# Channel attention and selective scan: the next image's statistics taken in the v stretch, its factors and key weights moved forward, B loaded ahead of C, one square per piece

## The chip, the cores and the metric

The kernel runs on one core of one Trainium2 chip. The time is the device time of one execution in microseconds. Three runs of the kernel before gave 19570.98, 19573.84 and 19581.24 us; the median, 19573.84, is the time before. The core has five engines that run their own instruction streams in order: PE (matmul), DVE (vector), ACT (activation), POOL (GpSimd) and SP, which here issues the DMAs.

## What is computed

The input x is 8 images of 384 channels and 64 x 64 positions (L = 4096), in float32. Two layers with residuals follow one another; the whole reference, cut to what matters:

```python
x = x + attention(gn(x))      # gn: 32 groups of 12 channels, over positions too
x = x + scan_layer(gn(x))

def attention(x):             # wq, wk, wv, wproj: 1x1; dw*: 3x3 for each channel
    q, k, v = (dwconv(conv1x1(x, w), dw) for ...)
    q, k = l2norm(q), l2norm(k)                      # over positions
    attn = softmax(q @ k.T * temperature)            # 8 heads, 48 x 48 each
    return conv1x1(attn @ v, wproj)

def scan_layer(x):            # 4 directions, 16 states for each channel
    dt, B, C = split(x_proj @ direction(x))
    dt = softplus(dt_proj @ dt + dt_bias)
    h[l] = h[l-1] * exp(dt * A) + dt * x * B
    y = sum over states of h * C, + D * x            # merged over directions
    return gelu(layernorm_over_channels(y) * ln_w + ln_b)
```

## The kernel before, in words

The images run one after the other (L1232): `channel_attention(b)`, then `selective_scan(b)`. The last part of an image, layer norm, gelu and residual, is done inside the next image's attention (`finishing`, L187), and for the last image at the end (`finish`). Channels are three blocks (NJ = 3) of 128 partitions. Most compute instructions are pinned: each engine executes them in the order in which they are written. DMAs are not pinned; a scheduler places them on SP's queue, and SP executes that queue in order.

**Attention.** Work is cut into 36 pieces (w, m, p): 12 of k, 12 of q (block m, then quarter p of 16 rows), 12 of v (quarter p, then block m); KQ = 24 is the number of the first v piece. The loop at L645 is a software pipeline over t: PE makes the bands of piece t+2 (L364, L368), ACT and POOL start and end the sum of piece t+1 (L416, L423), DVE finishes piece t with five taps and an addition (`finish_sum`, L440), and a finished k or q piece t-1 is transposed (`to_tokens`, L461). There ACT copies the transposes out of PSUM and squares the half piece with a running sum into `ssq` (L475). From t = KQ + 3 on the v stretch also projects: `project_in` (L595) on PE and `project_out` (L604) on DVE: add to x, take statistics, store x1. What is still to be projected after the loop is done at L736. `bank` (L341) hands out four PSUM banks in turn.

**Norms.** Group norm is folded into the weights: `norm_factors` (L131) aggregates batch statistics, averages mean and then variance over groups by two sets of seven matmuls with one column (L143), and ends with Sqrt on ACT and a reciprocal. `scale_weights` (L256) scales a weight matrix by rstd; `shift_of` (L263) makes a bias by nine matmuls with one column.

**Scan.** It has S = 32 steps (4 directions x 8 chunks of 512 positions), each UN = 12 units (3 blocks x 4 groups of 4 states), U = 384 units. In a unit ACT makes four decays (`decay`, L890, in three PSUM banks), POOL makes the product dt x B (`drive`, L903), DVE scans four states (`scan`, L913), PE transposes the result (`turn`), ACT copies it out (`keep`), PE multiplies by C (`add_up`). For every step PE projects x to dt, B and C (`project`, L802), and `lay_out` (L815) stores B and C to DRAM and loads C back in another shape (`cx`, four DMAs); `fetch` (L852) loads B to all partitions, one DMA of 1 MB for each group. C is shuffled by POOL (`mingle_c`), transposed by PE (`turn_c`) and spread by DVE (`spread_c`, L844). `project` and `turn_c` use one PSUM bank, tag "m". `drive(0)` and `drive(1)` are called ahead of the first unit, and unit u calls `drive(u + 1)`.

**Look-ahead.** In the last three steps of an image's scan (not of the last image) `look_ahead` (L1030) loads the next image's x in eight parts into the tile "near", takes 24 batch statistics on DVE (L1040), runs the steps of `norm_factors`, and two units before the end scales the key weights and makes their bias (L1054). Step 31 also loads x itself for the next image (L1160).

Of the kernel before, what the change touches and what calls it, by code (L numbers as in the profile page):

```python
# [9 lines left out]
F32 = mybir.dt.float32  # L10
# [85 lines left out]
def tile_channel_attention_then_selective_scan(ctx: ExitStack, tc: tile.TileContext, a: dict):  # L96
# [33 lines left out]

    def norm_factors(pool, psum, stats, tag, bank, pin=lambda i: i, **home):  # L131

        mv = pool.tile([P, NJ, 2], F32, name=f"mv{tag}", **home)
        mean = pool.tile([P, NJ], F32, name=f"mean{tag}", **home)
        rstd = pool.tile([P, NJ], F32, name=f"rstd{tag}", **home)
        var = pool.tile([P, NJ], F32, name=f"var{tag}", **home)

        def average(name, src):
            pm = psum.tile([P, CH], F32, tag=bank, name=f"{name}{tag}")
            for j in range(NJ):  # L140
                near = [i for i in range(NJ) if abs(i - j) <= 1]
                for i in near:
                    pin(nc.tensor.matmul(  # L143
                        pm[:, j : j + 1], lhsT=avg[:, i, j * P : (j + 1) * P], rhs=src[:, i, 0:1],
                        start=i == near[0], stop=i == near[-1],
                    ))
            return pm

        for j in range(NJ):
            pin(nc.vector.bn_aggr(mv[:, j, :], stats[:, j].rearrange("p c s -> p (c s)")))  # L150
        yield
        pm = average("pm", mv)
        yield
        pin(nc.vector.tensor_copy(mean, pm[:, 0:NJ]))
        pin(nc.vector.tensor_sub(var, mv[:, :, 0], mean))
        pin(nc.vector.tensor_mul(var, var, var))
        pin(nc.vector.tensor_add(var, var, mv[:, :, 1]))
        yield
        pv = average("pv", var.rearrange("p (j o) -> p j o", o=1))
        yield  # L160
        pin(nc.vector.tensor_scalar_add(rstd, pv[:, 0:NJ], GN_EPS))
        yield
        pin(nc.scalar.activation(rstd, rstd, AF.Sqrt))
        yield
        pin(nc.vector.reciprocal(rstd, rstd))
        yield mean, rstd
# [96 lines left out]
    def shift_of(pool, psum, tag, wt, mean, name):  # L263

        pin = tc.keep_in_program_order
        pb = psum.tile([P, CH], F32, tag=tag, name=f"pb{name}")
        for m in range(NJ):
            for j in range(NJ):
                pin(nc.tensor.matmul(
                    pb[:, m : m + 1], lhsT=wt[:, j, bass.ts(m, P)], rhs=mean[:, j : j + 1],  # L270
                    start=j == 0, stop=j == NJ - 1,
                ))
        bias = pool.tile([P, NJ], F32, name=f"bias{name}")
        pin(nc.vector.tensor_scalar_mul(bias, pb[:, :NJ], -1.0))
        return bias
# [20 lines left out]
    def channel_attention(b, x, stats, before):  # L296

        pin = tc.keep_in_program_order
        with ExitStack() as st:
# [9 lines left out]
            for n in ("k", "q", "v"):  # L309
                dws[n] = wp.tile([P, NJ, 9], F32, name=f"dw{n}{b}")  # L310
                nc.sync.dma_start(dws[n], a["dw" + n])
            mask = wp.tile([P, NJ, BW], F32, name=f"mask{b}")
            nc.sync.dma_start(mask, a["mask"])
# [13 lines left out]
            kT = wp.tile([P, NT, C], F32, tag="kv", name=f"kT{b}")  # L327
            ssq = wp.tile([P, 2 * NJ, NCH], F32, name=f"ssq{b}")
            ga = wp.tile([P, NJ, BW], F32, name=f"ga{b}")
            x1_d = dram.tile([NJ, P, L], F32, tag="x1d", bufs=2, name=f"x1d{b}")  # L330
# [130 lines left out]
            def to_tokens(t, h):  # L461
# [7 lines left out]
                if w == "k":  # L469
                    out = kT[:, n : n + 4, bass.ts(m, P)]  # L470
                else:
                    out = qTs[t, h] = work.tile([P, 4, P], F32, tag="qT", name=f"qT{b}_{t}_{h}")
                pin(nc.scalar.copy(out, pt))
                i = m if w == "k" else NJ + m
                pin(nc.scalar.activation(  # L475
                    src, src, AF.Square, accum_out=ssq[:, i, 2 * p + h : 2 * p + h + 1]
                ))

# [34 lines left out]
            def norms():  # L513

                polish_root(helper, roots, var)
                rks = work.tile([P, 4, P], F32, tag="qT", name=f"rks{b}")
                spread.append(rks.rearrange("p i l -> p (i l)"))
                rks = spread[0]
# [120 lines left out]
            def fin_bank(i, n):  # L639
                return bank(f"pz{b}_{i}_{n}")  # L640

            load_w("wq")
            parts = list(range(L // FT)) if before else []
            stats_left, todo, grams, last, ready = list(parts), [], [], iter(()), []
            for t in range(-2, T):  # L645
# [48 lines left out]
                def mid(tap):  # L694
# [4 lines left out]
                    if tap in (2, 8) and ready and t > KQ + 3:  # L699
                        project_out(*ready.pop(0))  # L700

                half(0)
# [22 lines left out]
                while ready:  # L725
                    project_out(*ready.pop(0))
                if t == KQ:
                    squares()
# [4 lines left out]
                if 0 <= cc < T and pieces[cc][:2] == ("v", NJ - 1):  # L733
                    p = pieces[cc][2]
                    todo += [(m, c) for c in (2 * p, 2 * p + 1) for m in range(NJ)]
            for m, c in todo:  # L736
                project_in(m, c)
                project_out(m, c)
                next(last, None)
                next(last, None)  # L740
            all_of(last)
        return x, x1_d, stats1

    def selective_scan(b, x1, stats1):

        y_d = dram.tile([L, C], F32, tag="yd", bufs=2, name=f"yd{b}")
        with ExitStack() as st:
# [18 lines left out]
            with tc.tile_pool(name=f"sn{b}", bufs=1, reuse_waits="tile") as np_:  # L766
                mean, rstd = all_of(norm_factors(np_, ps_t, stats1, f"1_{b}", "t", pin))
                shift = np_.tile([P, NJ], F32, name=f"shift{b}")
                nc.vector.tensor_mul(shift, mean, rstd)
                nc.vector.tensor_scalar_mul(shift, shift, -1.0)  # L770
                for c in range(5):
                    for j in range(NJ):
                        s = x1[j][:, bass.ts(c, CH)]
                        if c < 1:
                            pin(nc.scalar.activation(
# [39 lines left out]
            def lay_out(s):  # L815
# [3 lines left out]
                bc_d = dram.tile([2 * N, CH], F32, tag="bcd", bufs=3, name=f"bcd{b}_{s}")  # L819
                nc.sync.dma_start(bc_d, xd[R:XR, :])  # L820
                cx = work.tile([NG * NQ, NV, HP], F32, tag="cx", bufs=1, name=f"cx{b}_{s}")
                for g in range(NG):
# [3 lines left out]
                    )  # L826
                xds[s], bc_ds[s], cxs[s] = xd, bc_d, cx

# [179 lines left out]
            for j in range(NJ):  # L1008
                step_size(0, j, step_matmul(0, j))
                weigh(0, j)  # L1010
            for g in range(NG):
                fetch(0, g)
            mingle_c(0)
            turn_c(0)
            for g in range(NG):
                spread_c(0, g)
            drive(0)
# [12 lines left out]
            def look_ahead(u):  # L1030

                i = u - (U - 3 * UN)
                if b + 1 == B or i < 0:
                    return
                n, odd = divmod(i, 2)
                if i == 0:
                    near["st"] = x_stats(b + 1)
                if not odd and 1 <= n <= NCH:
                    for j in range(NJ):
                        pin(nc.vector.bn_stats(near["st"][:, j, n - 1, :], near["x"][:, j, :]))  # L1040
                if not odd and n < NCH:
                    near["x"] = big.tile([P, NJ, CH], F32, tag="near", name=f"nx{b}_{n}")
                    nc.sync.dma_start(
                        near["x"], x_d[b + 1, :, :, bass.ts(n, CH)].rearrange("j p l -> p j l")
                    )
                if i == 2 * UN + 1:
                    near["f"] = norm_factors(big, ps_m, near["st"], f"0_{b + 1}", "m", pin)
                if i > 2 * UN:
                    r = next(near["f"], None)
                    if r:  # L1050
                        near["r"] = r
                if i == 2 * UN:
                    near["w"] = load_wk(b + 1)
                if i == 3 * UN - 2:  # L1054
                    mean, rstd = near["r"]
                    scale_weights(near["w"], rstd)
                    bias = shift_of(big, ps_m, "m", near["w"], mean, f"{b + 1}k")
                    near["r"] += near["w"], bias

# [96 lines left out]
            for u in range(U + 1):  # L1156
                look_ahead(u)
                unit(u)
                if u == U - UN + 3 and b + 1 < B:
                    x_next = load_x(b + 1)  # L1160
            add_up(U - 1, NLB - 1)
            take(S - 1, 2)
            if x_next:
                x_next = x_next, near["r"]
        return y_d, x_next
# [60 lines left out]
    with tc.tile_pool(name="pm", bufs=1, space=PSUM) as ps:  # L1226
        st0 = all_of(norm_factors(big, ps, st0, "0_0", "m"))
        wk = load_wk(0)
# [3 lines left out]
    for b in range(B):  # L1232
        x1, x1_d, stats1 = channel_attention(b, *x, before)
        y_d, x = selective_scan(b, x1, stats1)
        before = (b, x1_d, y_d)
# [50 lines left out]
```

## Time and profile before

| what | value |
| --- | --- |
| time, median of three runs | 19573.84 us (19570.98 to 19581.24) |
| profiled execution, its own time | 19593.03 us |
| span of its instructions | 19591.2 us |
| mean granted TensorE clock | 0.954 |
| DMA | 1849.25 MB, mean 94 GB/s |
| statistics of x1, L607, DVE 128x512 | 192, 694 ns each |
| statistics of the next x, L1040, DVE 128x512 | 168, 672 ns each |
| ACT table loads at L872 | 256, 1283 ns each |
| POOL product, L910, 128x2048 | 3072, 4578 ns each |
| DVE scan, L922, 128x512, with a carry | 10752, 1263 ns each |

Times are those of one profiled execution. A row of groups gives the engine, the operation, its tiles (out<-in), its count, busy time and mean duration. A row of the timeline gives the start, the duration and, in brackets, how long the engine had been idle before it and what ended that idle time. A row of windows gives each engine's busy time in a stretch.

### The profile page before, as it was taken

Reading aid. Unit: us, or ns where it says so; the run is one execution under the profiler, and the core shown is the slowest. Engines: PE = TensorE matmul, PEld = TensorE weight load, DVE = VectorE, ACT = ScalarE, POOL = GpSimd, SP = SyncE. Lnnn points to the kernel's source line nnn. Section 1 sums busy time; section 2 is a strip of 40 time slices with the busy share of each in tenths; the row PEclk is TensorE's granted clock in tenths of the full one; section 3 lists DMA queues with packets and bytes.
Section 4 is the critical chain, followed back from the end, with each engine's and each line's share of the span. In section 5 each row is a group of like instructions: output and inputs, shape, how many; then the busy total and the mean of one; then the engine's idle time right before and its main releaser. Section 6 shows DMA issues by size and latency. Waiting matters only on the chain.

```text
span 19591.2 us, 415258 instructions
## 1 busy us (share of the span) xinstructions
PE 17097.0 (87%) x166560; PEld 10219.2 (52%) x166560; DVE 18453.4 (94%) x17510; ACT 17584.1 (90%) x30011; POOL 16874.4 (86%) x7486
## 2 busy tenths in 40 slices
PE   7888888888888888888888888888888888888887
PEld 4555545555455554555545555455554555545554
DVE  7999989999899998999989999899998999989998
ACT  6999979999799987999879998899988999889998
POOL 4999959999599985999859998599985999869997
PEclk9999999999999999999999999999999999999998
DMA  1232322223222232232322323223232223322223
GB/s 47 84 97 97 112 89 83 94 97 111 91 86 94 95 109 89 87 97 96 109 85 87 97 97 108 85 87 97 97 108 92 83 95 97 106 93 88 94 93 124
DMA packets 1214410, 1849.25 MB, mean 94 GB/s; under 512 B 154209, under 2 KB 1018721, under 8 KB 1075265
## 3 DMA queue, kind: packets, MB, share of 16 engines
q1 hardware_dynamic: 1211616, 1822.57, 28.7%
q8 instruction: 1314, 21.53, 0.5%
q14 instruction: 616, 5.04, 0.1%
q10 hardware_dynamic: 864, 0.12, 0.0%
HBM read 1503.58 MB, written 318.77 MB: 93 GB/s over the span
## 4 chain that ended last, share of the span: by engine, by line
ACT 27%; PE 23%; DVE 15%; issue 4%; POOL 3%; DMA 1%; SPq 0%; DVEq 0%; ACTq 0%; POOLq 0%
ACT da L898 12%; ACT hc L949 10%; PE pt L943 10%; DVE h L922 10%; PE py L960 5%; PE px L810 3%; DVE ac L451 3%; POOL db L910 2%; ACT dt L872 1%; PE pp L599 1%; PE pd L864 1%; PE py L966 1%; ACT pr L413 1%; ACT L872 1%; ACT L898 1%
## 5 line engine op out<-in xcount | busy, mean ns | idle before, releaser
L910 POOL TENSOR_TENSOR db<-w,B 128x2048 f32<-128x2048 f32 x3072 | 14053.0, 4578 | 618.8 <-DVE h L922 514.7
L922 DVE TENSOR_TENSOR_SCAN h<-da,ca,db 128x512 f32<-128x512 f32 x10752 | 12786.6, 1263 | 305.3 <-ACT da L898 287.0
L898 ACT ACTIVATE da<-dt,neg_a 128x512 f32<-128x512 f32 x12288 | 8741.8, 713 | 157.6 <-DVE h L922 153.4
L943 PE MATMUL pt<-ident,h 128*128 128x128 f32 x49152 | 8127.0, 294 | 858.4 <-DVE h L922 505.8
L949 ACT COPY hc<-pt 128x512 f32<-128x512 f32 x12288 | 7393.0, 604 | 704.7 <-PE pt L943 641.1
L943 PEld LDWEIGHTS pt<-ident,h 128*128 128x128 f32 x49152 | 5452.3, 146 | 3314.2 <-issue 1912.0
L960 PE MATMUL py<-hc,cp 128*32 128x128 f32 x98304 | 5070.4, 290 | 893.4 <-ACT hc L949 726.0
L960 PEld LDWEIGHTS py<-hc,cp 128*32 128x32 f32 x98304 | 2050.1, 110 | 3164.5 <-ACT hc L949 1607.1
L922 DVE TENSOR_TENSOR_SCAN h<-da,db 128x512 f32<-128x512 f32 x1536 | 1748.2, 1206 | 115.8 <-ACT da L898 73.5
L420 POOL TENSOR_TENSOR pr<-pr,pr 128x1008 f32<-128x1008 f32 x288 | 673.3, 2338 | 1201.1 <-ACT pr L413 1184.0
L810 PE MATMUL px<-x,wx 128*44 128x128 f32 x6144 | 1219.8, 343 | 36.9 <-DVE cp L849 21.3
L881 POOL TENSOR_TENSOR w<-x,dt 128x512 f32<-128x512 f32 x744 | 1062.4, 1428 | 33.4 <-ACT dt L872 31.9
L810 PEld LDWEIGHTS px<-x,wx 128*44 128x44 f32 x6144 | 687.4, 128 | 367.0 <-issue 190.0
L864 PE MATMUL pd<-xd,wdt 128*128 128x512 f32 x1536 | 731.8, 613 | 157.0 <-DVE h L922 151.2
L426 POOL TENSOR_TENSOR pr<-pr,pr 128x1008 f32<-128x1008 f32 x288 | 574.8, 1996 | 277.2 <-ACT pr L413 193.8
L849 DVE TENSOR_TENSOR cp<-quad,pct 128x512 f32<-128x512 f32 x1024 | 628.2, 674 | 10.9 <-PE pct L838 10.9
L599 PE MATMUL pp<-v,mT 128*128 128x512 f32 x1152 | 539.1, 618 | 92.5 <-DVE v L456 91.4
L872 ACT ACT_TABLE_LOAD x256 | 328.4, 1283 | 229.1 <-PE pd L864 228.1
L936 POOL COPY ca<-h 128x4 f32<-128x4 f32 x2688 | 531.6, 198 | 0.0
L864 PEld LDWEIGHTS pd<-xd,wdt 128*128 128x128 f32 x1536 | 272.3, 190 | 465.4 <-issue 239.2
L872 ACT ACTIVATE dt<-pd,dt_bias 128x512 f32<-128x512 f32 x768 | 475.0, 686 | 8.2 <-PE pd L864 4.4
L1002 DVE TENSOR_TENSOR ys<-ys,py 128x512 f32<-128x512 f32 x576 | 383.9, 667 | 34.6 <-PE py L960 34.6
(334 smaller groups left out, 11500.5 us busy)
## 6 DMA issues: line engine op xcount, KB each, us to landing
B<-bcd SPq DMA_DIRECT2D x1024, 1024.0 KB, 4.8
yd<-ys SPq DMA_DIRECT2D x384, 256.0 KB, 3.4
ys<-yd SPq DMA_DIRECT2D x768, 128.0 KB, 2.9
yd<-ys SPq DMA_DIRECT2D x768, 128.0 KB, 4.3
x<-in_x SPq DMA_DIRECT2D x48, 1024.0 KB, 7.2
x1d<-x SPq DMA_DIRECT2D x192, 256.0 KB, 2.8
ys<-yd SPq DMA_DIRECT2D x192, 256.0 KB, 3.0
fy<-yd SPq DMA_DIRECT2D x128, 384.0 KB, 3.8
```

The source lines that it names most:

```text
L420: pin(nc.gpsimd.tensor_add(q[:, :, 1:], q[:, :, 1:], left[:, :, : W - 1]))
L599: pin(nc.tensor.matmul(pps[m, c], lhsT=fold_of[0][:, j, bass.ts(m, P)], rhs=vs["v"][:, j, bass.ts(c, CH)], start=j == 0, stop=j == NJ - 1,))
L810: pin(nc.tensor.matmul(split(pxs[s][:XR, :])[:, part, :], lhsT=wx[:, j, k, :], rhs=view(x1[j], k, c)[:, part, :], start=i == 0, stop=i == ...
L864: pin(nc.tensor.matmul(pd, lhsT=wdt[:, k, bass.ts(j, P)], rhs=xds[s], start=True, stop=True))
L872: pin(nc.scalar.activation(dts[s, j], pd, AF.Softplus, bias=small["dt_bias"][:, j, k : k + 1]))
L881: pin(eng.tensor_mul(split(ws[s, j]), view(x1[j], k, c), split(dts[s, j])))
L898: pin(nc.scalar.activation(t, dts[s, j], AF.Exp, scale=neg_a[:, j, steps[s][0], n : n + 1]))
L910: pin(eng.tensor_mul(t, w.broadcast_to([P, NV, CH]), bts[s, g]))
L922: pin(nc.vector.tensor_tensor_scan(h, da, db, 0.0 if start else carries[s - 1][:, j, n : n + 1], ALU.mult, ALU.add,))
L943: pin(nc.tensor.transpose(t[:, f, :], hs[u][:, bass.ts(q, HP), :].rearrange("p l v -> p (l v)"), ident))
L949: pin(nc.scalar.copy(t, pts.pop((u, lb))))
L960: pin(nc.tensor.matmul(py[f * HP : (f + 1) * HP, lb, :], lhsT=cps[s, g][:, q, :], rhs=hc[:, f, :], start=g == lb == 0, stop=g == NG - 1 an ...
```

## The change

There are six edits.

1. In the v stretch of image b, x of image b + 1 is loaded in twelve parts of 1024 columns into two tiles that have no more use by then (`qT`, and `gm`, which joins the former `mask` and `ga`), and DVE takes the statistics from there, at taps 0 and 6 of `finish_sum`.
2. The factors of image b + 1 are made step by step between the last projections of image b. `norm_factors` now keeps one operand of each small subtraction and product in PSUM.
3. The key weights of image b + 1 are loaded at unit 24 by the text, scaled at unit 41 and their bias made at unit 42. What `look_ahead` did in the last three steps is gone. The load of x itself stays.
4. At the start of the scan B's first group is loaded before C's four loads, and C is spread after unit 0.
5. The first chunk's middle block is normalised by DVE, the others still by ACT; the shift is one operation, not two.
6. A piece is squared once (1024 columns), not in two halves. The q transposes stand in one tile with two halves, where they had two buffers.

```diff
-    def norm_factors(pool, psum, stats, tag, bank, pin=lambda i: i, **home):
+    def norm_factors(pool, bank, stats, tag, pin=lambda i: i):
...
-        pin(nc.vector.tensor_copy(mean, pm[:, 0:NJ]))
-        pin(nc.vector.tensor_sub(var, mv[:, :, 0], mean))
-        pin(nc.vector.tensor_mul(var, var, var))
-        pin(nc.vector.tensor_add(var, var, mv[:, :, 1]))
+        off = pm[:, NJ : 2 * NJ]
+        pin(nc.vector.tensor_sub(off, mv[:, :, 0], pm[:, :NJ]))
+        pin(nc.vector.tensor_copy(var, off))
+        pin(nc.vector.tensor_mul(off, var, off))
+        pin(nc.vector.tensor_add(var, mv[:, :, 1], off))
+        pin(nc.vector.tensor_copy(mean, pm[:, :NJ]))
...
                 pin(nc.scalar.copy(out, pt))
-                i = m if w == "k" else NJ + m
-                pin(nc.scalar.activation(
-                    src, src, AF.Square, accum_out=ssq[:, i, 2 * p + h : 2 * p + h + 1]
-                ))
+                if h:
+                    i, src = m if w == "k" else NJ + m, piece_out(t)
+                    pin(nc.scalar.activation(src, src, AF.Square, accum_out=ssq[:, i, p : p + 1]))
...
+            ahead = [(j, c) for j in range(NJ) for c in range(0, NCH, 2)] if b + 1 < B else []
+            st0, coming = x_stats(b + 1) if ahead else None, []
+            halls = [qT.rearrange("p i l -> p (i l)"), gm[:, : 2 * CH]]
+
+            def load_ahead():
+
+                for t in halls:
+                    if ahead:
+                        j, c = ahead.pop(0)
+                        nc.sync.dma_start(t, x_d[b + 1, j, :, c * CH : (c + 2) * CH])
+                        coming.append((j, c, t))
+
+            def stats_ahead():
+
+                if coming:
+                    j, c, t = coming.pop(0)
+                    for i in range(2):
+                        pin(nc.vector.bn_stats(st0[:, j, c + i, :], t[:, bass.ts(i, CH)]))
...
+                    if tap in (0, 6):
+                        stats_ahead()
...
+                if t > KQ + 2:
+                    load_ahead()
...
+            while coming:
+                stats_ahead()
+            factors = iter(())
+            if st0:
+                factors = norm_factors(big, bank, st0, f"0_{b + 1}", pin)
+            after = None
             for m, c in todo:
                 project_in(m, c)
+                after = next(factors, after)
                 project_out(m, c)
...
+            for after in factors:
+                pass
...
-                nc.vector.tensor_mul(shift, mean, rstd)
-                nc.vector.tensor_scalar_mul(shift, shift, -1.0)
+                pin(nc.vector.scalar_tensor_tensor(shift, mean, -1.0, rstd, ALU.mult, ALU.mult))
...
-                        if c < 1:
+                        if c < 1 and j != 1:
...
                 nc.sync.dma_start(bc_d, xd[R:XR, :])
+                xds[s], bc_ds[s] = xd, bc_d
+                if s == 0:
+                    fetch(0, 0)
                 cx = work.tile([NG * NQ, NV, HP], F32, tag="cx", bufs=1, name=f"cx{b}_{s}")
...
-            for g in range(NG):
+            for g in range(1, NG):
                 fetch(0, g)
             mingle_c(0)
             turn_c(0)
-            for g in range(NG):
-                spread_c(0, g)
...
-                if not odd and 1 <= n <= NCH:
-                    for j in range(NJ):
-                        pin(nc.vector.bn_stats(near["st"][:, j, n - 1, :], near["x"][:, j, :]))
-                if not odd and n < NCH:
-                    near["x"] = big.tile([P, NJ, CH], F32, tag="near", name=f"nx{b}_{n}")
-                    nc.sync.dma_start(
-                        near["x"], x_d[b + 1, :, :, bass.ts(n, CH)].rearrange("j p l -> p j l")
-                    )
-                if i == 2 * UN + 1:
-                    near["f"] = norm_factors(big, ps_m, near["st"], f"0_{b + 1}", "m", pin)
...
-                if i == 2 * UN:
+                if u == 2 * UN:
                     near["w"] = load_wk(b + 1)
-                if i == 3 * UN - 2:
-                    mean, rstd = near["r"]
-                    scale_weights(near["w"], rstd)
-                    bias = shift_of(big, ps_m, "m", near["w"], mean, f"{b + 1}k")
-                    near["r"] += near["w"], bias
+                if u == 3 * UN + 5:
+                    scale_weights(near["w"], after[1])
+                if u == 3 * UN + 6:
+                    near["b"] = shift_of(big, ps_m, "m", near["w"], after[0], f"{b + 1}k")
...
                 unit(u)
+                if u == 0:
+                    for g in range(NG):
+                        spread_c(0, g)
```

## The prediction

> **What bounds the kernel now.** I read the page first (busy shares, chain, groups), then one image stage by stage in the table of windows, then the waits and the timelines at the four places that the change touches. I use image 2 (the third) and, as a witness, image 7 (the last), which has no next image.
>
> ```profile
> span 19591.2 us, 415258 instructions
> PE 17097.0 (87%) x166560; PEld 10219.2 (52%) x166560; DVE 18453.4 (94%) x17510; ACT 17584.1 (90%) x30011; POOL 16874.4 (86%) x7486
> 5382.40:7000.00 1617.60, 1439.37 (x15981) 879.14 (x15981) 1579.84 (x1432) 1527.99 (x2655) 1566.97 (x693) 0.97 0.29 93
> ```
> Window columns: stretch, length, busy us of PE, weight load, DVE, ACT, POOL (instructions), clock, DMA share, GB/s. Inside the scan DVE works 1579.84 of 1617.60 us: it sets the pace, POOL is close behind (1566.97), so a DVE microsecond there is a microsecond of time. An image lasts some 2438 us: keys 87, queries 107, values and projection 194, start of the scan 26, scan 2020.
>
> ```profile
> 7117.80:7189.10 71.30, 57.66 (x639) 34.26 (x631) 71.30 (x72) 62.92 (x108) 61.62 (x30) 0.98 0.46 143
> 7189.10:7255.10 66.00, 53.36 (x576) 31.71 (x575) 65.01 (x64) 57.30 (x98) 60.43 (x28) 0.97 0.42 135
> 7255.10:7330.00 74.90, 62.56 (x636) 41.22 (x634) 65.36 (x61) 59.61 (x105) 54.05 (x16) 0.83 0.29 91
> 19305.60:19367.00 61.40, 54.74 (x607) 31.99 (x607) 60.76 (x56) 58.28 (x104) 60.79 (x29) 1.00 0.31 97
> 19367.00:19429.50 62.50, 56.24 (x603) 33.37 (x599) 61.07 (x56) 58.08 (x103) 61.37 (x31) 0.95 0.31 95
> 19429.50:19487.90 58.40, 48.57 (x594) 29.10 (x592) 58.40 (x52) 55.20 (x97) 48.19 (x13) 0.97 0.09 20
> ```
> These are the last three scan steps of image 2 (71.3 + 66.0 + 74.9 = 212.2) and of image 7 (182.3). Image 7 has no look-ahead. The other six images lie between 210 and 213 by the starts of their scans.
>
> **Removed at the scan's end.** The difference, 29.7 us, is the price of the look-ahead where it stands. It agrees with its parts: 24 statistics x 0.672 = 16.1, aggregation 0.8, small operations 6.6 (one of 128x3 takes 5.74), about 2.6 behind Sqrt and its two table loads, 5.0 behind the key bias.
>
> ```profile
> 7275.77 5.74 DVE L155 TENSOR_TENSOR var<-mv,mean 128x3 f32<-128x3 f32 x1
> 7303.43 2.46 DVE L922 TENSOR_TENSOR_SCAN h<-da,ca,db 128x512 f32<-128x512 f32 x2 [2.61 <-ACT da L898]
> 7325.76 0.16 DVE L274 TENSOR_SCALAR bias3k<-pb3k 128x3 f32<-128x3 f32 x1 [4.98 <-PE pb3k L269]
> ```
> Once it is gone POOL is next, and image 7 already includes that. So -29.7 (bounds -27 and -30), seven times. The loads of x at L180 remain; the eight loads at L1043 go from SP's queue, and no DVE wait of these steps names them.
>
> **Key weights, moved to the fourth step.** Scaling costs ACT 3 x 0.57 = 1.7 us; two of its decays are ready ahead, which hides it. The nine bias matmuls took PE 4.15 us, and DVE stands at L274 until they end, with all scans of that unit behind it. Of the 4.98 us, 1.2 was PE waiting for the scaled weights, which now happens a unit earlier. That leaves 3.8 + 0.16, and something for ACT's copies held behind PE: +4.5 (2 to 6). The weight load stands where the first x load stood.
>
> **Statistics in the v stretch.** Twelve pairs of 1.35 us, ahead of taps 0 and 6 of six pieces, two pieces of which have no projection beside them.
>
> ```profile
> 5178.14 0.69 DVE L606 TENSOR_TENSOR x<-x,pp 128x512 f32<-128x512 f32 x1 [3.22 <-PE pp L599]
> 5183.94 0.69 DVE L606 TENSOR_TENSOR x<-x,pp 128x512 f32<-128x512 f32 x1 [1.91 <-PE pp L599]
> 5202.55 0.69 DVE L606 TENSOR_TENSOR x<-x,pp 128x512 f32<-128x512 f32 x1 [3.10 <-PE pp L599]
> 5208.35 0.69 DVE L606 TENSOR_TENSOR x<-x,pp 128x512 f32<-128x512 f32 x1 [1.91 <-PE pp L599]
> 5217.13 0.69 DVE L606 TENSOR_TENSOR x<-x,pp 128x512 f32<-128x512 f32 x1 [1.03 <-PE pp L599]
> 5222.61 0.69 DVE L606 TENSOR_TENSOR x<-x,pp 128x512 f32<-128x512 f32 x1 [1.59 <-PE pp L599]
> 5241.16 0.69 DVE L606 TENSOR_TENSOR x<-x,pp 128x512 f32<-128x512 f32 x1 [3.05 <-PE pp L599]
> 5246.64 0.69 DVE L606 TENSOR_TENSOR x<-x,pp 128x512 f32<-128x512 f32 x1 [1.66 <-PE pp L599]
> ```
> PE is the bound here, and each bracket is idle time of DVE just behind a statistics pair. Carrying DVE's lateness along: first piece 3.22 and 1.91 cover both pairs; the second has no gap, 2.7 late; third 2.7 + 1.35 - 3.10 = 0.95, then 0.4; fourth 0.7, then 0.5; fifth 3.2; sixth 1.5, then 1.2. After that DVE works without a gap to the last v piece, on which PE waits, so 1.2 us come out. I take +2 for a bank that a late sum holds; if the cover were gone it would be 16.1, so bounds 0 and 8.
>
> The twelve x loads (512 KB) share SP's queue with stores and with the loads that finish the previous image. Each waits for the statistics that still read its hall, and whatever follows on SP waits with it (up to 1.5 us by the places of the instructions). Reading to reuse is one piece, 9 to 15 us; B, twice as large, lands in 4.8 us. DMA share there is 0.6 to 0.7, so there is room.
>
> **Factors in the projection's tail.** DVE's part (0.8 + about 1.0 + 0.3) fits in its waits for the projection; Sqrt falls to an idle ACT, one table load already standing there. PE's 14 small matmuls lie on the path, since PE works without a gap from 5271.92 to 5288.7. Here a rule decides the price. In rows just after a PE wait the two averages cost 2.52 and 3.15 us. The Trainium skill, "TensorE: Matmul & The Clock Gate", "What's actually happening", has the array at half clock after an idle window and at full clock after some 3.4 us of work. The trace agrees: after the 7.6 us gap the second result comes 4.4 us after the first, the next ones every 2.58. The new matmuls stand after the second, so they are warm: 1.72 each, the row of the scan's end. Sum 3.4 by the rule, 5.7 by the rows of the cold places; I take +3.5 (1.5 to 6).
>
> **Start of the scan.** B's first group now goes out ahead of the four C loads, 1.8 us earlier.
>
> ```profile
> 5313.51 2.29 DVE L910 TENSOR_TENSOR db<-w,B 128x2048 f32<-128x2048 f32 x1
> 5324.91 10.39 DVE L922 TENSOR_TENSOR_SCAN h<-da,db 128x512 f32<-128x512 f32 x9 [4.36 <-POOL db L910]
> ```
> The first product could start near 5311.4; POOL's next (issued twice, before the loop and in unit 0) follows it, so unit 1 starts some 1.7 us sooner, and the four C spreads (2.48 us), put behind unit 0, lie in the 4.36 us wait. Two things speak against it. The Trainium skill, "SBUF — State Buffer", "SBUF: two separate sides", lets a DVE operation with two SBUF inputs and a reading GpSimd operation block each other: POOL's C shuffle, done before the product now, would come behind it (0.4 us; without the rule nothing; the 5.74 us row above looks like this block). And PE's projection for step 1 needs the bank that the spreads read: it stands at PE's head until about 5323, with unit 0's transposes (5320.6 now) behind it. With 0.2 us for the merged shift, and one x norm moved from ACT to DVE that leaves PE's first operand where it was: -1 (-2 to +3).
>
> **One square per piece.** 2 x (0.63 + 0.19) becomes about 1.14 + 0.19: 0.3 us of ACT, 24 times an image. DVE binds these stretches (103.24 of 107.20 us in the queries) and waits 1.5 us for ACT in image 2, so nearly nothing; image 0 waits about 5.5 beyond its start. -3 in all.
>
> **Sum.** Per image -29.7 + 4.5 + 2 + 3.5 - 1 = -20.7; times seven -145; image 7's start -1, squares -3: -149. The profiled execution took 19593.0 (its span 19591.2); less 149 is 19444. The median of the runs is 19573.8, 19 below; less 149 gives 19425.
>
> **The rivals.**
> 1. *The statistics stay exposed* in the v stretch, because PE's banks wait for late sums, so DVE's 16.1 us pass through: -29.7 + 4.5 + 16.1 + 3.5 - 1 = -6.6, times seven and the rest: -50, 19524. For it: two of six pieces have no gap. Against: the eight gaps above.
> 2. *The x loads come late and DVE waits at tap 0 and tap 6*: a slower kernel. Ten of twelve loads are reloads into a hall; SP executes in order, so one wait there holds the next load. At w us each the image pays 10w; above about 2.1 us it turns, at 4 us it is +40 - 20.7 = +19, times seven, less 4: +131, 19705. For it: SP alternates with waits on DVE and ACT. Against: 9 to 15 us of reach against about 5.
> 3. *More is hidden*: the key bias costs 2, statistics nothing, factors 2, start -2: -27.7 per image, about -198, 19376.
> 4. *The end does not shrink*, since something else (the x load, POOL) holds those steps: +4.5 + 2 + 3.5 - 1 = +9 per image, 19633. Image 7 speaks against it.
>
> **How the numbers follow.** Forecast 0.70, rival 1 0.13, rival 2 0.04, rival 3 0.11, rival 4 0.02. A measurement of this kernel tells about 0.2%, 39 us, from no change. Rival 1 lies on that border, so half of it counts as same: faster 0.88, same 0.06, slower 0.06. The range, 19385 to 19525, goes from -26 to -6 us per image, most of the forecast's bounds and half of each of rivals 1 and 3.
>
> **What would show it.** Last three steps of images 0 to 6 at 182 to 184 us; a fourth step near 66.5 with a DVE wait of 4 us at the bias; v and projection of images 1 to 6 longer by 5 to 6 us than image 7's; bn statistics without DMA waits; the first scan earlier and step 0 shorter or equal. It is wrong if the v stretch grows by over 10 us or DVE waits there for DMA.

## The result and the profile after

The changed kernel takes 19437.57 us (median of 4 runs, 19435.2 to 19452.52), beside 19572.41 for the kernel before, run beside it (4 runs, 19568.36 to 19581.24). The ratio is 0.9932, 95% interval 0.992 to 0.9943: 135 us less. The profiled executions, with which all that follows is read, took 19452.52 and 19593.03: 140.5 less.

The head of the page of the changed kernel: DVE still carries the kernel.

```profile
span 19450.7 us, 414947 instructions
...
PE 17034.3 (88%) x166560; PEld 10177.3 (52%) x166560; DVE 18413.2 (95%) x17526; ACT 17504.7 (90%) x29605; POOL 16881.1 (87%) x7486
```

Windows of image 2 (columns as in the prediction): v stretch with projection, step 3, and the last three steps of the scan.

```profile
5052.90:5251.10 198.20, 166.66 (x532) 84.58 (x530) 168.58 (x216) 129.50 (x195) 89.88 (x47) 0.93 0.49 163
5462.10:5529.10 67.00, 59.64 (x642) 38.19 (x645) 61.46 (x58) 60.27 (x106) 60.96 (x29) 0.92 0.24 77
7087.60:7149.60 62.00, 55.63 (x607) 32.90 (x607) 60.67 (x56) 58.07 (x103) 60.63 (x29) 0.97 0.31 96
7149.60:7212.70 63.10, 56.81 (x607) 33.55 (x606) 61.28 (x56) 58.33 (x103) 61.24 (x29) 0.95 0.38 125
7212.70:7271.40 58.70, 47.58 (x592) 28.74 (x592) 56.25 (x50) 54.47 (x97) 46.54 (x13) 1.00 0.28 94
```

The last three rows sum to 183.8 where they were 212.2. Cutting every image at its first key matmul, first v matmul, last x1 statistic and first scan of each step gives this balance of the two profiled executions (us, all eight images unless said; "rest" is what lies before the first key matmul and in image 7's other stages):

| stage | forecast | measured |
| --- | --- | --- |
| last three steps, images 0 to 6 | -208 | -205 |
| step 3, images 0 to 6 | +31.5 | +32.8 |
| v and projection, images 0 to 6 | +38.5 | +37.1 |
| start of the scan and step 0 | -8 | -12.3 |
| steps 1 and 2 | 0 | -6.2 |
| keys and queries | -3 | -10.9 |
| steps 4 to 28 | 0 | +22.2 |
| rest | 0 | +1.9 |
| sum | -149 | -140.5 |

Four places of image 2 show how. In the v stretch DVE's waits for the projection, in the part shown before, have shrunk from eight, of 1 to 3.2 us, to four, of 0.5 to 2.0; and one statistics pair waits for its load (2.10 us; image 4 has the longest such wait, 4.39, in the second fence).

```profile
5135.04 0.69 DVE L610 TENSOR_TENSOR x<-x,pp 128x512 f32<-128x512 f32 x1 [2.03 <-PE pp L603]
5140.85 0.69 DVE L610 TENSOR_TENSOR x<-x,pp 128x512 f32<-128x512 f32 x1 [0.86 <-PE pp L603]
5165.26 0.69 DVE L610 TENSOR_TENSOR x<-x,pp 128x512 f32<-128x512 f32 x1 [0.63 <-PE pp L603]
5179.51 0.69 DVE L610 TENSOR_TENSOR x<-x,pp 128x512 f32<-128x512 f32 x1 [0.49 <-PE pp L603]
5198.17 1.29 DVE L663 BATCH_NORM_STATS2 st<-qT 128x6 f32<-128x512 f32 x2 [2.10 <-DMA qT<-in_x]
```

```profile
10033.28 1.29 DVE L663 BATCH_NORM_STATS2 st<-qT 128x6 f32<-128x512 f32 x2 [4.39 <-DMA qT<-in_x]
```

In the tail the two sets of small matmuls take 1.62 us each on PE (1.72 in the forecast), at a granted clock of 1.00 in all seven images. In step 3 DVE stands at the key bias:

```profile
5236.04 1.62 PE L144 MATMUL pm<-mv,avg 128*128 128x1 f32 x14
5242.75 1.62 PE L144 MATMUL pv<-var,avg 128*128 128x1 f32 x14
```

```profile
5494.39 0.16 DVE L277 TENSOR_SCALAR bias3k<-pb3k 128x3 f32<-128x3 f32 x1 [3.00 <-PE pb3k L272]
```

At the start of the scan the product follows B's landing at once, and unit 1 starts 30.65 us after the last x1 statistic (34.8 before). Image 2 gains most here: from the last x1 statistic to the end of step 0 it is 5.0 us shorter, the other images between 4.1 shorter and 0.8 longer.

```profile
5269.99 2.29 DVE L950 TENSOR_TENSOR db<-w,B 128x2048 f32<-128x2048 f32 x1 [2.28 <-DMA B<-bcd]
5270.81 1.73 POOL L872 COPY cy<-cx 64x128 f32<-64x128 f32 x1 [20.13 <-DMA cx<-bcd]
...
5281.46 1.48 PE L847 MATMUL px<-x,wx 128*44 128x128 f32 x6 [8.49 <-DVE cp L889]
5281.73 5.89 DVE L962 TENSOR_TENSOR_SCAN h<-da,db 128x512 f32<-128x512 f32 x5 [0.42 <-POOL db L950]
```

### The profile page after: what moved, and what is told of

It is laid out like the page before. It is cut to its first block, busy times and chain, and to the rows that moved or that the text cites. A ratio compares the mean times of both kernels' runs of the same rounds, so it can differ in the third digit from the quotient of the medians.

```text
span 19450.7 us, 414947 instructions
## 1 busy us (share of the span) xinstructions
PE 17034.3 (88%) x166560; PEld 10177.3 (52%) x166560; DVE 18413.2 (95%) x17526; ACT 17504.7 (90%) x29605; POOL 16881.1 (87%) x7486
## 4 chain that ended last, share of the span: by engine, by line
ACT 37%; PE 33%; DVE 18%; issue 6%; POOL 4%; DMA 1%; SPq 0%; DVEq 0%; ACTq 0%; POOLq 0%
ACT da L938 15%; PE pt L983 14%; ACT hc L989 14%; DVE h L962 12%; PE py L1000 7%; PE px L847 5%; DVE ac L457 4%; POOL db L950 4%; ACT dt L912 2%; PE pp L603 2%; ACT pr L419 1%; PE pd L904 1%; PE py L1006 1%; ACT L912 1%; ACT L938 1%
## 5 line engine op out<-in xcount | busy, mean ns | idle before, releaser
L962 DVE TENSOR_TENSOR_SCAN h<-da,db 128x512 f32<-128x512 f32 x1536 | 1749.1, 1206 | 102.3 <-ACT da L938 89.9
```

What stands on the lines that cost most here:

```text
L962: pin(nc.vector.tensor_tensor_scan(h, da, db, 0.0 if start else carries[s - 1][:, j, n : n + 1], ALU.mult, ALU.add,))
```

## The experiments

The theory was the prediction's own sum; its rivals put the cost elsewhere in each place. Stage numbers below are those of the cut above. Edits are to the changed kernel, except one; "..." marks lines of an edit that are left out. The whole-kernel ratios of most versions have intervals that overlap that of the changed kernel (0.992 to 0.9943), so the verdicts rest on the stages of one profile each.

Stages that an edit does not touch differ from profile to profile too, and the granted clock goes with it. In the kernels with one square per piece, keys and queries of images 1 to 7 last 192.9 to 193.5 us at a granted clock of 0.99 or 1.00 and 196.2 to 197.0 at 0.974. In this table each row gives how far versions with that stage's code unchanged lie from the changed kernel's profile, as a sum over the images. This is called the spread below; a difference inside it shows nothing by itself.

| stage | versions with the same code |
| --- | --- |
| v and projection, images 0 to 6 | -4.4 to +2.9 |
| step 3, images 0 to 6 | -6.6 to 0 |
| start of the scan and step 0 | -6.8 to +3.9 |
| steps 1 and 2 | -0.9 to +2.3 |
| keys and queries | -6.6 to +3.9 |

**The key bias: the negation a unit later.**

```diff
-                    near["b"] = shift_of(big, ps_m, "m", near["w"], after[0], f"{b + 1}k")
+                    near["pb"] = shift_matmuls(ps_m, "m", near["w"], after[0], f"{b + 1}k")
+                if u == 3 * UN + 7:
+                    near["b"] = shift_bias(big, near["pb"], f"{b + 1}k")
```

> The changed kernel, with DVE's negation of the key bias put one unit behind its nine matmuls (unit 43, not 42). In the changed kernel step 3 lasts 66.5 to 67.9 us in images 0 to 6 and 63.4 in image 7. Theory (DVE stands at the bias until PE is through, and the scans stand behind it): step 3 falls to 63 to 64 in images 0 to 6, the DVE wait at the bias is gone, about -25 us in all, 19413. Rival (the cost is PE's 4.15 us or ACT's scaling, which only shows at the bias): step 3 stays at 66 to 67, 19437.

Measured: 19425.98 (ratio 0.9918, 0.9904 to 0.9933). Step 3 stayed at 65.0 to 67.8 in images 0 to 6, 4.4 less in sum, which is inside the spread. At the same granted clock, 0.92, it lasts 66.5 us in both versions. The theory fell. PE, ACT and DVE of image 2:

```profile
5491.90 4.00 PE L278 MATMUL pb3k<-mean,wk 128*128 128x1 f32 x18
5496.95 0.59 ACT L1000 COPY hc<-pt 128x512 f32<-128x512 f32 x1 [4.24 <-PE pt L994]
5498.16 1.29 DVE L973 TENSOR_TENSOR_SCAN h<-da,ca,db 128x512 f32<-128x512 f32 x1 [3.83 <-ACT da L949]
```

DVE no longer waits at the bias, yet it waits 3.83 us for a decay. The block of small matmuls holds the transposes behind it; ACT waits for them at its copy; the decay stands behind the copy in ACT's queue. The other rival, ACT's scaling, is small: after it DVE waits 0.25 us for a decay.

**The key bias in three parts.** Three of the nine matmuls each in units 5, 6 and 7, the scaling in unit 3, the negation in unit 8.

```diff
...
+                if s == 3 and 5 <= r < 8 and b + 1 < B:
+                    if r == 5:
+                        near["pb"] = ps_m.tile([P, CH], F32, tag="m", name=f"pb{b + 1}k")
+                    shift_part(near["pb"], near["w"], after[0], r - 5)
                 turned(2)
```

> The nine matmuls of the key bias no longer stand as one block ahead of unit 6 of step 3: three each go into units 5, 6 and 7 (behind the transposes' first half, where the projections of the next step stand in units 0 to 3), the scaling goes two units earlier and the negation opens unit 8. The theory left by the first experiment: the 4.0 us block on TensorE holds the transposes behind it, so ACT's copy of a transposed state waits (4.24 us in that run) and the decays behind it in ACT's queue come late for DVE. Cut in three, each block is 1.3 us, which the two decays that are ready ahead cover: step 3 of images 0 to 6 falls from 66.5 to 67.9 to about 63 to 64.5, in sum -15 to -24 us. Rival: TensorE has no spare time in those units, so the 4 us pass through wherever they stand: step 3 stays at 66 to 68.

Measured: 19416.89 (0.9916, 0.9899 to 0.9932). Step 3 fell to 61.5 to 63.9, -32.9 in sum: all that it had grown by. The theory holds, but more came off than it said (-15 to -24), and the granted clock rose with it. The parts run at 1.00:

```profile
5491.99 0.73 PE L278 MATMUL pb3k<-mean,wk 128*128 128x1 f32 x6
5496.47 0.73 PE L278 MATMUL pb3k<-mean,wk 128*128 128x1 f32 x6
5501.40 0.73 PE L278 MATMUL pb3k<-mean,wk 128*128 128x1 f32 x6
```

In the nine versions that leave the block whole, a stretch at half clock of 3.4 to 10.2 us overlaps the block, or begins at most 1.1 us behind it, in every image; in the two versions with three parts there is none at that place. Step 3 without the matmuls (kernel before, image 4), in three parts (image 0), as a block (`after_sbuf`, image 0), then in three parts (image 1) and as a block (changed kernel, image 0); the clock is the third number from the end:

```profile
10382.60:10446.10 63.50, 56.09 (x624) 34.90 (x624) 61.09 (x56) 58.87 (x103) 60.67 (x29) 0.95 0.25 82
636.60:700.50 63.90, 57.76 (x641) 36.81 (x641) 61.27 (x58) 60.01 (x106) 60.48 (x29) 0.95 0.24 81
637.70:703.40 65.70, 58.48 (x645) 37.00 (x645) 61.21 (x58) 60.38 (x106) 59.70 (x29) 0.95 0.23 79
3047.00:3108.70 61.70, 55.47 (x649) 35.16 (x644) 60.86 (x58) 60.20 (x107) 59.56 (x28) 1.00 0.25 84
635.30:703.10 67.80, 61.37 (x641) 39.73 (x645) 61.21 (x57) 60.19 (x106) 60.26 (x29) 0.90 0.24 76
```

At equal clock (0.95) the block costs some 2 us and the parts some 0.4. The rest of the 4.7 us goes with the lower clock. This edit also moved the scaling, so the share of that move is not separated.

**The x loads left out**; the statistics read one of the two tiles as it is, so that the factors of images 1 to 7 are not those of x.

```diff
-            halls = [qT.rearrange("p i l -> p (i l)"), gm[:, : 2 * CH]]
+            halls = [qT.rearrange("p i l -> p (i l)")] * 2
...
-                        nc.sync.dma_start(t, x_d[b + 1, j, :, c * CH : (c + 2) * CH])
```

> The twelve loads of the next image's x in the v stretch are left out, and the statistics read what lies in one of the two halls (so the statistics of images 1 to 7 are not those of x; all else is computed as before). Theory: each image from 1 to 6 loses time to one load that comes late (DVE waits of 10.7 us in sum, 4.39 in image 4, about 1.3 in the others), and only to that: v and projection of image 4 falls from 201.5 to about 197.5, of the other images by 1 to 1.5, in sum -8 to -11 us, the whole kernel by as much. Rival: DVE waits for TensorE there anyway in the next taps, so that the wait for the load costs less than it lasts: v and projection falls by under 0.5 in images 1, 2, 3, 5 and 6.

Measured: 19422.35 (0.9916, 0.9901 to 0.9931). V and projection: 197.3 in image 4 (201.5 with the loads), 0.1 to 0.8 less in images 1, 2, 3, 5 and 6, -6.7 in sum. So it lies between the two: waits of 0.9 to 2.1 us cost 0.1 to 0.8. Part of the 4.1 of image 4 goes with the clock, 0.924 there and 0.931 in images 1, 2, 3, 5 and 6. Nor is its wait a fixed price of image 4: in `bias_late`, which has all the loads, images 3 to 5 have no such wait and last 197.1 to 197.3. The -6.7 is only 2.3 beyond the spread.

**Loads and statistics left out**, the factors computed from image 0's statistics.

```diff
-            st0, coming = x_stats(b + 1) if ahead else None, []
+            st0, coming = first if ahead else None, []
...
-                        nc.sync.dma_start(t, x_d[b + 1, j, :, c * CH : (c + 2) * CH])
-                        coming.append((j, c, t))
```

> The loads of the next image's x and its 24 statistics are both left out of the v stretch; the factors in the projection's tail are still computed, from the first image's statistics (so images 1 to 7 are normalized with those of image 0). Theory, by the prediction's sum: the factors cost 3.5 us of the 5.3 that v and projection grew by, the statistics the rest: v and projection of images 1 to 6 at 196.5 to 197.5 without the loads and statistics (before 193.0 to 194.3), image 0 at about 187 (before 183.4, after 193.6), in sum over the images about -13 to -18 against the changed kernel. Rival: the factors are nearly free beside the projection (1 us) and the statistics carry the cost: v and projection at 194 to 195, image 0 at 184.5, in sum -27 to -32.

Measured: 19444.18 (0.9925, 0.991 to 0.994); v and projection -14.2 in sum, image 0 at 187.9, images 1 to 6 at 196.2 to 197.5. The theory holds: the factors alone add 22.9 in sum to the kernel before (3.0 an image in images 1 to 6, 4.5 in image 0). With the run before this splits the +37.1 of this profile: factors 22.9, statistics 7.5, late loads 6.7, each uncertain by a few us. Of the statistics 5.7 are image 0's, which has no previous image to finish and fewer gaps (DVE idles 34.3 us of that stretch before the change, 40.7 in image 1); the other six pay 0.3 each.

**The x loads issued from ACT's queue.**

```diff
-                        nc.sync.dma_start(t, x_d[b + 1, j, :, c * CH : (c + 2) * CH])
+                        nc.scalar.dma_start(t, x_d[b + 1, j, :, c * CH : (c + 2) * CH])
```

> The twelve loads of the next image's x are issued from ACT's queue in place of SP's, at the same place of the program. Theory: the load that comes late does so because SP stands at a load of the finishing of the previous image ahead of it, in order; from ACT's queue it goes out as soon as the statistics have left the hall, the DVE waits for x (10.7 us in sum) go, and v and projection of images 1 to 6 falls by 1 to 4 us, in sum -8 to -11. Rival: ACT is held in its turn, at the wait for the statistics that still read the hall, with its copies of the projection behind it, and v and projection grows by as much or more; or the transfer itself is what is slow, and the waits stay.

Measured: 19441.0 (0.9923, 0.9908 to 0.9938); v and projection +15.2. The rival holds. ACT's queue reaches the loads later than SP's (in image 3 the eighth to eleventh load go out at 7592.89, 7602.48, 7608.15 and 7616.45, against 7583.03, 7590.55, 7596.85 and 7608.35, where the statistics as a whole begin 2.4 us later), and the statistics now wait 18 times instead of 6. The view of the line that issues the loads:

```profile
L655 ACTq EVENT_SEMAPHORE  x84: 17/38/7425, 278.5 to 14864.6; - x84
...
who waited for it (us, times):
  DVE st L663: 23.7, 18
```

**POOL's second product issued once.**

```diff
             drive(0)
-            drive(1)
```

> The changed kernel without the second of the two identical products for unit 1 (the call ahead of the loop is left out; unit 0 makes it). Theory (with C spread behind unit 0, DVE reaches unit 1 only when the scans of unit 0 and the four spreads are done, and these wait for ACT's decays): unit 1 starts at most 0.5 us earlier, start and step 0 together stay at 88 to 90 us for each image, -3 us in all, 19434. Rival (POOL's doubled product still decides when unit 1 starts, as it did in the kernel before): -4.5 us for each of 8 images, -36 in all, 19402.

Measured: 19454.53 (0.9932, 0.9915 to 0.9949); start and step 0 +3.1 over eight images, inside the spread, so no gain: the doubled product does not decide.

**C loaded and spread in the old order.**

```diff
-                if s == 0:
-                    fetch(0, 0)
...
-            for g in range(1, NG):
+            for g in range(NG):
                 fetch(0, g)
             mingle_c(0)
             turn_c(0)
+            for g in range(NG):
+                spread_c(0, g)
```

> The changed kernel with B behind C and the spreads ahead of unit 0 again, as before; the merged shift and the x norm on DVE stay. Start and step 0 together are 90.5 us (mean of 8 images) in the kernel before and 89.0 in the changed one. Theory (the 1.5 us come from this edit): 90.4, 19449. Rival (they come from the merged shift, the moved norm or a warmer PE, and B first is worth nothing since POOL's shuffle is held and PE's transposes start late): 89, 19438.

Measured: 19448.37 (0.9929, 0.9914 to 0.9944); start and step 0 +13.2, steps 1 and 2 +5.9, both clear of the spread. The theory holds: the edit (B first and the later spreads together) is worth 2.4 us an image. The clock moves with it: in start and step 0 it is 0.814 on average in this version and in the kernel before, 0.830 in the changed kernel. Where the clock is equal (0.81) the stages last 89.9 to 90.9 us in all three, so that what the edit saves comes with the higher clock.

**Two squares per piece**, as before.

```diff
-                if h:
-                    i, src = m if w == "k" else NJ + m, piece_out(t)
-                    pin(nc.scalar.activation(src, src, AF.Square, accum_out=ssq[:, i, p : p + 1]))
+                i = m if w == "k" else NJ + m
+                pin(nc.scalar.activation(
+                    src, src, AF.Square, accum_out=ssq[:, i, 2 * p + h : 2 * p + h + 1]
+                ))
```

> The changed kernel with two half squares for each piece again. Keys and queries together are 195.9 us (mean of 8 images) in the kernel before and 194.6 in the changed one, and the difference is between -4.6 and +3.5 from image to image. Theory (DVE binds, ACT's 0.3 us a piece are hidden, except in image 0): keys and queries of image 0 back to about 195, the others within 1 us, 19441. Rival (the whole -10.9 us of these stretches is due to the squares): 19448.

Measured: 19452.05 (0.993, 0.9915 to 0.9945); keys and queries of image 0 +4.9, all eight +5.5. These sums mix the edit with the clock: image 0 stood at 1.00 in the changed kernel and at 0.974 in this run. At equal clock every image gains: images 1 to 7 last 193.9 to 194.6 us at 0.991 with two squares (three versions) and 192.9 to 193.5 with one. So the edit is worth about 1 us an image, not image 0's alone, and DVE does not hide it as the theory had it. Image 1 of this run and image 2 of the changed kernel, both at 0.99:

```profile
2455.50:2649.70 194.20, 173.49 (x633) 95.26 (x630) 176.64 (x186) 172.42 (x269) 97.42 (x45) 0.99 0.13 42
4859.40:5052.90 193.50, 173.14 (x632) 95.07 (x629) 176.38 (x186) 168.62 (x227) 97.28 (x45) 0.99 0.14 42
```

**The kernel before with the new small operations alone.**

```diff
-        pin(nc.vector.tensor_copy(mean, pm[:, 0:NJ]))
-        pin(nc.vector.tensor_sub(var, mv[:, :, 0], mean))
+        off = pm[:, NJ : 2 * NJ]
+        pin(nc.vector.tensor_sub(off, mv[:, :, 0], pm[:, :NJ]))
...
```

> The kernel before, with only the new form of the small operations in the norm factors (mean and mean square taken from PSUM, with the products kept there). It tests the reading of the 5.74 us row at the scan's end. Theory: that operation was held because both its inputs lay in SBUF while a GpSimd operation was reading there; with one input in PSUM it takes 0.2 to 0.3, and the last three steps of images 0 to 6 fall from 210 to 212 to about 205 to 207, in sum -35 to -40 us. Rival: the operation waited for something else (ACT, or the work queued on DVE itself), or the time comes back in the next wait because POOL is the one that binds there: the three steps stay at 210 to 212, or fall by under 2.

Measured: 19522.25 (0.9969, 0.9957 to 0.9981), 62 us less than the kernel before, run beside it; the last three steps, up to the last scan, 203.6 to 204.6, -52.1 in sum. The theory holds, with more than expected. POOL in the kernel before, around the 5.74 us operation that starts at 7275.77:

```profile
7272.47 9.02 POOL L910 TENSOR_TENSOR db<-w,B 128x2048 f32<-128x2048 f32 x2
```

The two products end at 7281.49; the DVE operation ends at 7281.51. So it is in all seven images: one or two small operations are held, each ends 0.02 us after a product, and they take 5.5 to 6.4 us together. With an operand in PSUM (before, new form) it runs in the middle of three products:

```profile
7252.44 13.62 POOL L912 TENSOR_TENSOR db<-w,B 128x2048 f32<-128x2048 f32 x3
7255.50 0.15 DVE L155 TENSOR_TENSOR pm<-mv,pm 128x3 f32<-128x3 f32 x1
```

**The changed kernel with the old small operations**: the reverse of that edit, in the changed kernel.

> The changed kernel with the small operations of the norm factors in their old form (mean copied to SBUF first, difference, square and sum there). In the kernel before, the new form alone gave 52 us over the ends of seven scans, because GpSimd was multiplying there. Theory: in the projection's tail GpSimd does nothing while these operations run, so the old form costs the same 0.8 us there, no row lasts over 0.3 us, and v and projection and the whole stay as in the changed kernel (within 10 us): the move itself takes away the block, and the new form adds nothing to it. Rival: something on GpSimd holds them there too (up to 6 us an image): v and projection grows by 3 to 6 us, the whole by 20 to 40.

Measured: 19432.77 (0.992, 0.9904 to 0.9937); v and projection -1.0 in sum, no small operation over 0.17 us. In the tail POOL is idle, so the form does not matter there: the move alone removes the block.

**The version that the runs pointed to**: bias in three parts, and each x load issued when the statistics of its tile have been.

```diff
...
                         pin(nc.vector.bn_stats(st0[:, j, c + i, :], t[:, bass.ts(i, CH)]))
+                    load_ahead(t)
...
```

> The version that the runs so far point to: the key bias in three parts as in the run before, and each load of the next image's x issued from SP's queue as soon as the statistics of its hall have been issued (at tap 0 and tap 6), in place of both at the end of the piece. SP then stands ahead of the loads of the finishing, with half a piece to a whole piece more from issue to reading. Theory: the DVE waits for x (10.7 us in sum) go, v and projection of images 1 to 6 comes to 197.0 to 197.5 as without the loads (sum -5 to -7 against the changed kernel), step 3 stays at 61.5 to 64 (sum -33), the whole about -40: near 19400. Rival: SP, which now waits at each load for DVE's statistics, holds the loads and stores of the finishing and of the projection behind it, and v and projection grows by 2 us or more in images 1 to 6.

Measured: 19402.88 (4 runs, 19379.54 to 19414.48; 0.9903, 0.9887 to 0.992). Step 3 gave -29.4, v and projection -4.2 (image 4 at 197.7), which is inside the spread. It is the fastest version run, but its median lies only 14 us below the one with the bias in parts alone, and the intervals of the two overlap. The DVE waits for x are 7.6 us in six places, not zero, and just as long with the loads left where they were (`spread_bias`: 7.6 us, six places). So the earlier issue is not shown to help: the late load still stands behind a load of the finishing in SP's queue (image 2), though its tile has been read by 5181.46.

```profile
5184.81 0.36 SPq L214 DMA_DIRECT2D fy<-x1d  x1
5185.23 0.48 SPq L664 DMA_DIRECT2D qT<-in_x  x1
```

## Why the prediction was right, and where its steps were not

The mechanism and the size were right: the look-ahead's removal gave 29.3 us an image (29.7 forecast), and image 7, the witness, stayed at 183 (182.2 before). The rivals fell: the statistics are not exposed (rival 1; 0.3 us in six of seven images), and the end did shrink (rival 4). The prediction's own signs of being wrong came up in part: the v stretch of image 0 grew by 10.2 us (over 10 was the sign), and DVE waits for DMA in six images. That the sum held all the same is in part luck, as misses in both directions cancel. Six steps need correction.

- *Key weights, +4.5.* The size was right (4.7; 3.7 to 4.5 in other versions with the block whole), the path only half. The wait at the bias is what the trace shows, but it is not the cause: take it away and the time stays. I had "something for ACT's copies held behind PE" as a remainder; it is a path of its own that keeps the time, and cutting the block in three takes the cost away. Some 2.7 of the 4.7, an estimate from the rows at equal clock, goes with the lower clock at the block, for which I had no term. The 4.15 us that I took for the nine matmuls was itself a price at a granted clock of 0.57 (in image 1 of the kernel before: 2.73 us at 1.00), so the agreement in size is partly luck.
- *Statistics, +2, bounds 0 and 8.* Images 1 to 6 pay 0.3. I carried DVE's lateness gap by gap, which was too careful there, and I took image 2 for all: image 0 has no finishing, and grew by 5.7 for its statistics.
- *The x loads.* "There is room" was wrong for one load in each of six images: rival 2 on a small scale, 1.1 us an image in this profile. The bandwidth was there; the place in SP's queue was not. This +6.7 and the statistics' +7.5 happen to sum to the 14 that I had given to the statistics alone.
- *Factors, +3.5.* Measured 3.0 in images 1 to 6. The warm price held against the cold one: 1.62 us at a granted clock of 1.00 in the new place, 3.15 at 0.50 in the averages of x1's variance (images 1 and 3).
- *Start, -1.* Start and step 0 give -1.5 an image, steps 1 and 2 -0.8, for which I had nothing; both come with a higher clock. POOL's shuffle behind DVE's product took 1.73 us where its median is 0.41, and it ends 0.26 us behind that product, so the block that I named agrees with the trace. It costs unit 1 at most the 0.42 us for which DVE waits there, since the spreads of C hold DVE until then.
- *Squares, -3.* I put the gain at nearly nothing outside image 0, because DVE binds; at equal clock it is about 1 us in each image, some 8 in all.

Steps 4 to 28 have identical code and take 22 us longer over the eight images, more than the whole gap of 8.5 between forecast and sum. The granted clock, which I had not looked at there, goes with it. In one kernel (before), the same steps of images 4 and 5:

```profile
10446.10:12005.40 1559.30, 1390.22 (x15324) 845.00 (x15324) 1518.94 (x1376) 1467.29 (x2551) 1506.95 (x664) 0.96 0.29 94
12887.70:14435.10 1547.40, 1378.98 (x15331) 834.88 (x15335) 1516.26 (x1377) 1465.91 (x2552) 1506.61 (x664) 0.98 0.29 95
```

Over the eight images of all 13 profiles, 0.01 of granted clock goes with 8 us of these steps (correlation -0.96). The mean is 0.9699 before and 0.9671 after; by that slope, an estimate, 18 of the 22 us go with it. The five steps that grew most (6, 7, 13, 16 and 24, by 0.4 to 0.7 us each) are steps whose clock fell, by 0.010 to 0.017. In eleven profiles of versions of the changed kernel the sum lies between 12435 and 12463 us, in the two of versions of the kernel before at 12428 and 12412.

What stays open is why the clock falls where it does, and whether it lengthens a stage or follows from the same wait as the length. No run holds one of them fixed.

## What to carry to other kernels

A wait that the trace prints on the binding engine can be the second of two paths from one block; before moving the waiter, shorten the block: small matmuls in a row hold every later transpose, and through an in-order engine the decays behind it. Before two versions are compared by stage, compare the granted clock of the stage: here it moves step 3 by more than 2 us with the same instructions. A load with bandwidth to spare is late when its queue stands at another wait, and a change of queue helps only if the new engine reaches the place sooner. Tiny vector operations with two SBUF inputs should not stand beside long GpSimd operations (here 5.74 us, against 0.15 with one operand in PSUM): put one operand into PSUM, or move them to where GpSimd rests.

## What the runs showed that I had not expected

- The small operations alone were worth 52 of the 205 us at the scan's end (7.4 an image, more than the 5.74 of the one row), and 62 of the whole kernel's time where all six edits gave 135: in the kernel before the first of them lasts up to 6361 ns, and the one behind it up to 4436, with medians of 163 and 161. The Trainium skill, "SBUF — State Buffer", "SBUF: two separate sides", describes such an exclusive lock of DVE and GpSimd; the end times, equal to 0.02 us, agree, and that the PSUM form escapes it is shown here.
- The same nine matmuls with one column last 4.00 us in images 0, 3 and 4 of the changed kernel, 2.33 to 2.50 in the others, and 2.2 in three parts. The granted clock tells them apart: 0.50, 0.84 to 0.90, and 1.00. Their records start every 213 ns at 0.50 and every 112 ns at 1.00.
- With a megabyte sent ahead the small loads behind it land later: in image 2, C's take 3.8 to 4.4 us behind B, against 1.65 to 2.29 at the same place of the kernel before.
